# Moving a quarter of each chunk's addition into y from VectorE to TensorE and ScalarE, in the scans of a two-layer kernel

## The chip, the core and the metric

The kernel runs on one core of a Trainium2 chip. The core has a matrix engine (PE, also TensorE; PEld is its loading of weights), a vector engine (DVE, VectorE), a scalar engine (ACT, ScalarE), a general engine (POOL, GpSimd) and a queue engine (SP, SyncE) that mostly starts DMAs. Each engine works through its own queue of instructions in order, and waits on semaphores for the others. The metric is the device time of one execution in microseconds (us). Data lies in SBUF (128 partitions), and TensorE writes its sums into PSUM, eight banks of 512 f32 values per partition.

## The reference, cut to what matters

Two layers run one after the other on an image batch x of 8 x 128 x 128 x 128 (images, height, width, channels). Layer 0 is a linear attention with a layer norm and a residual. Layer 1 projects each image to 256 channels, convolves it depthwise, and runs four selective scans (k = 0 to 3) over its L = 16384 tokens: in order, backwards, in turned order (rows and columns exchanged), and turned backwards. Per scan and channel the recurrence is:

```python
delta = softplus(delta + dbias)
du = delta * u
def step(xc, inp):
    dlt, dut, Bt, Ct = inp
    dA = exp(dlt * A)
    xc = dA * xc + dut * Bt
    return xc, xc * Ct          # D_STATE = 1
y = ys + u * Dv
...
y = y0 + y1 + y2 + y3           # each put back into token order
out = layernorm(y * silu(z)) @ Wout
```

The part that the change touches is the product with C (`xc * Ct`) and the sum of four scans into one y per image.

## The kernel before, in words

The program has three parts: `layer0`, `layer1_front` (projection, convolution, and the rows that make delta, B and C) and `layer1_scan`. Only the last is changed. It works on 512 "units": 8 output images x 4 slots (one scan each) x 16 chunks (`NCH`) of `CH` = 1024 tokens. A chunk has 256 channels, held as two halves c = 0, 1 of 128 partitions. Its tokens fall into two halves of 512 (`hf`). The sums of one image stand in the SBUF tile `y`.

What happens to chunk n, engine by engine:

- `delta(n, c)` (L973): TensorE makes delta for one half of the channels, two bf16 matmuls of 512 columns, into a PSUM tile `px` of two banks. There are three such tiles, taken in turn.
- `soften` (L977): ScalarE takes softplus of it into SBUF (`sp`). `decay` (L981): ScalarE writes exp(A x delta) back over the `px` tile. Softplus and exp lie in different tables of ScalarE, so that a step has two table loads.
- `weigh` (L996; L994 in some steps): POOL multiplies u by delta into `h`. There are two `h` tiles, each for both channel halves of one chunk.
- `scan` (L1004 backwards, L1006 forwards): VectorE runs the recurrence over 1024 tokens, in place in `h`, one instruction per channel half. It starts from the last column of the `h` of the chunk before.
- `spread` (L1012): TensorE spreads C's row over all 128 partitions, one bf16 matmul per token half, into a PSUM bank of its own (tags "pc" and "pt", one bank each).
- `emit(n, hf)`: VectorE multiplies h by C. In the first slot of an image (`place` 0) it writes y directly (L1024). In the other three slots one token half (`sl.first`, the half that holds the scan's last column, which the next chunk's scan still needs) goes into a `px` tile that has become free (L1034 where this slot's order of tokens is turned against y's, L1038 where it isn't), and the other half is multiplied in place in `h` (L1027).
- `gather` (L1046): VectorE adds the product in the `px` tile to y, both channel halves in one instruction.
- `add` (L1054): POOL adds the other token half from `h` to y, one instruction per channel half.

`step(n)` writes out by hand the order in which all this is issued, and `in_order` fixes it: on every engine, instructions run in the order of the text. Step n runs the scans of chunk n, emits chunk n - 1 and makes delta for chunk n + 1. On VectorE a step that only adds ("plain") is `emit`, `gather`, `emit`, `scan` c = 0, `scan` c = 1. On ScalarE it is decay 0, decay 1, softplus 0, softplus 1 (of the next chunk). On TensorE it is delta 0, delta 1, spread, spread. On POOL it is weigh 0, weigh 1, add, add.

While the first slot of the next image runs, the finished image leaves (`leaving`): its chunks are multiplied by the gate, normalised, projected and stored (`gate`, `square`, `moments`, `keep`, `to_tokens`, `square_mean`, `variance`, `deviation`, `project`, `store`), in the same steps. SP's queue starts the loads of u, z and of the rows, POOL's queue adds the u x D terms by DMA (L946).

Of the kernel before, what the change touches and what calls it, by code (L numbers as in the profile page):

```python
# [8 lines left out]
F32 = mybir.dt.float32  # L9
BF16 = mybir.dt.bfloat16  # L10
AF = mybir.ActivationFunctionType
ALU = mybir.AluOpType
# [4 lines left out]
P = 128  # L17
B = 8
H = W = 128
L = H * W  # L20
NH, HD = 4, 32
NC2 = 2
R = 8
K = 4
GW = 4
GN = GW * H
# [4 lines left out]
CH = 1024  # L31
# [757 lines left out]
def layer1_scan(ctx: ExitStack, tc, ubs, xps, zs, gs, dtw, dtb, a_log, gamma, beta, w_out, out):  # L789
# [15 lines left out]
    nc = tc.nc  # L805
    const = ctx.enter_context(tc.tile_pool(name="l2c", bufs=1))
    big = ctx.enter_context(tc.tile_pool(name="l2b", bufs=1))
    wp = ctx.enter_context(tc.tile_pool(name="l2w", bufs=3))
    sm = ctx.enter_context(tc.tile_pool(name="l2s", bufs=4))
    px = ctx.enter_context(tc.tile_pool(name="l2px", bufs=3, space=PSUM))  # L810
    pe = ctx.enter_context(tc.tile_pool(name="l2pe", bufs=1, space=PSUM))
# [14 lines left out]
    for dst, src, rows in ((wparts, dtw.rearrange("k r d -> r k d"), R), (bparts, dtb.rearrange("o (k d) -> o k d", d=D2), 1)):  # L826
        x = wp.tile([rows, K, D2], F32, name="w32", tag="sp", bufs=2)
        nc.sync.dma_start(x, src)
        q = wp.tile([rows, 3, K, D2], BF16, name="w16", tag="h", bufs=2)
# [12 lines left out]
    for i in range(3):  # L842
        t = const.tile([P, CH], BF16, name=f"rows{i}")
# [3 lines left out]
    for i in range(3):  # L847
        t = const.tile([P, D2], BF16, name=f"dtw{i}")
        nc.gpsimd.memset(t, 0.0)
        dws.append(t)  # L850
    csel = const.tile([P, P], BF16, name="csel")
    nc.gpsimd.memset(csel, 0.0)
    nc.gpsimd.memset(csel[96:99, :], 1.0)


    wg = const.tile([P, NC2, P], F32, name="wg")
# [4 lines left out]
    means = wp.tile([P, P], F32, name="means", tag="r", bufs=2)  # L861
    nc.vector.memset(means, 1.0 / (NC2 * P))

    mean = const.tile([P, 32], F32, name="mean2")
    nc.vector.memset(mean, 0.0)
    nc.vector.memset(mean[:, 0:1], 1.0 / (NC2 * P))
    sel = const.tile([P, NC2, 2], F32, name="sel")
    nc.vector.memset(sel, 0.0)
    for j in range(2):
# [65 lines left out]
    units = []  # L935
    for o in range(B):
        for s in ([3, 0, 1, 2] if o % 4 >= 2 else [1, 2, 3, 0]):
            sl = Slot(len(units) // NCH, o, s)
            units += [(sl, i) for i in range(NCH)]

    ubt, sp, da, hs, leaving = {}, {}, {}, {}, {}
# [22 lines left out]
    def delta(n, c):  # L964
        sl, i = units[n]
        rw = rws[n % 3]
        da[n, c] = p = px.tile([P, CH], F32, name="px")
        for hf in range(2):
            if sl.dt_turned_back:
                src = rw[:, (1 - hf) * 512 : (1 - hf) * 512 + 512][:, ::-1]  # L970
            else:
                src = rw[:, hf * 512 : hf * 512 + 512]
            nc.tensor.matmul(p[:, hf * 512 : hf * 512 + 512], sl.dw[:, c * P : c * P + P], src, start=True, stop=True)  # L973

    def soften(n, c):
        sp[n, c] = t = wp.tile([P, CH], F32, name="sp", tag="sp", bufs=2)
        nc.scalar.activation(t, da[n, c], AF.Softplus)  # L977

    def decay(n, c):
        sl, i = units[n]  # L980
        nc.scalar.activation(da[n, c], sp[n, c], AF.Exp, scale=sa[:, sl.s, c : c + 1])  # L981
# [16 lines left out]
    def scan(n, c):  # L998
        sl, i = units[n]
        x, e = da[n, c], hs[n][:, c, :]  # L1000
        last = 0 if sl.back else CH - 1
        start = 0.0 if i == 0 else hs[n - 1][:, c, last : last + 1]
        if sl.back:
            nc.vector.tensor_tensor_scan(e[:, ::-1], x[:, ::-1], e[:, ::-1], start, ALU.mult, ALU.add)  # L1004
        else:
            nc.vector.tensor_tensor_scan(e, x, e, start, ALU.mult, ALU.add)  # L1006

    cps, ts = {}, {}

    def spread(n, hf, tag):  # L1010
        cps[n, hf] = p = pe.tile([P, 1, GN], F32, name="pc", tag=tag)
# [2 lines left out]
    def emit(n, hf):  # L1014

        sl, i = units[n]
        h = hs[n][:, :, hf * 512 : hf * 512 + 512]
        c = cps.pop((n, hf)).to_broadcast([P, NC2, GN])  # L1020
        if sl.place == 0:
            v = sl.y_at(i, hf)
            split = "p c (a b) -> p c a b"
            nc.vector.tensor_tensor(v, h.rearrange(split, b=H), c.rearrange(split, b=H), ALU.mult)  # L1024
            return
        if hf != sl.first:
            nc.vector.tensor_tensor(h, h, c, ALU.mult)  # L1027
            return
        p = da.pop((n, 1))
        if sl.y_turned:  # L1030
            ts[n] = p.rearrange("p (c b a) -> p c b a", c=NC2, a=GW)
            t = p.rearrange("p (c b a) -> p c a b", c=NC2, a=GW)
            split = "p c (a b) -> p c a b"
            nc.vector.tensor_tensor(t, h.rearrange(split, b=H), c.rearrange(split, b=H), ALU.mult)  # L1034
        else:
            t = p.rearrange("p (c q) -> p c q", c=NC2)
            ts[n] = t.rearrange("p c (a b) -> p c a b", b=H)
            nc.vector.tensor_tensor(t, h, c, ALU.mult)  # L1038

    def gather(n):  # L1040

        sl, i = units[n]
        v = sl.y_at(i, sl.first)
        if sl.y_turned:
            v = v.rearrange("p c a b -> p c b a")
        nc.vector.tensor_tensor(v, v, ts.pop(n), ALU.add)  # L1046

    def add(n):
        sl, i = units[n]
        hf = 1 - sl.first  # L1050
        h = hs[n][:, :, hf * 512 : hf * 512 + 512].rearrange("p c (a b) -> p c a b", b=H)
        v = sl.y_at(i, hf)
        for c in range(NC2):
            nc.gpsimd.tensor_tensor(v[:, c], v[:, c], h[:, c], ALU.add)  # L1054


    zt, rst, pts, mv = {}, {}, {}, {}
# [8 lines left out]
    def fetch(o, m):  # L1066
        for hf in range(2):
            zt[m, hf] = z = wp.tile([P, NC2, GN], F32, name="z", bufs=6)
            p = mirrored(o, m, hf)
            nc.sync.dma_start(z, zs[o].rearrange("c p l -> p c l")[:, :, p * GN : p * GN + GN])  # L1070

    def gate(o, m, hf, eng):
        z, ym = zt[m, hf], piece(m, hf)
        eng.tensor_tensor(z, ym[:, :, ::-1] if o % 2 == 1 else ym, z, ALU.mult)  # L1074
# [28 lines left out]
        nc.scalar.activation(t, pts[m][:, :, :, 0], AF.Square)  # L1103

    def variance(m):
        rst[m] = rstd = sm.tile([P, GW, NC2], F32, name="rstd")
        nc.vector.tensor_tensor(rstd, pts.pop(m)[:, :, :, 1], mv.pop(m), ALU.subtract)  # L1107
        nc.vector.tensor_scalar(rstd, rstd, 0.0, EPS1, ALU.max, ALU.add)

# [27 lines left out]
    for o in range(B):  # L1137
        n = (o + 1) * K * NCH
        for j in range(NCH):
# [3 lines left out]
            q = j - LATE if j >= LATE else NCH - LATE + j  # L1143
# [7 lines left out]
    N = len(units)  # L1151

    def step(n):
        live = 0 <= n < N
        then = n + 1 < N
        before = 1 <= n <= N
        now, last, soon, later = (leaving.get(n + i) for i in (0, -1, 1, 2))
        first = before and units[n - 1][0].place == 0
        if before:
            half1 = units[n - 1][0].first  # L1160
            emit(n - 1, half1)
            if not first:
                gather(n - 1)
        if now and last:
            gate(*now, 1, nc.vector)
        if before:
            emit(n - 1, 1 - half1)
        if n + 2 < N:
            load_rows(n + 2)
        if n in fetched:  # L1170
            fetch(*fetched[n])
        if last:
            nc.scalar.preload_act_table_set("natural_log_exp_and_others")
        if live:
            decay(n, 0)
        if now:
            square(now[1], 1)
        if live:
            decay(n, 1)
        if last:  # L1180
            deviation(last[1])
        if live:
            weigh(n, 0)
            if n + 2 < N:
                load(n + 2, 0)
        if live:
            weigh(n, 1)
            if n + 2 < N:
                load(n + 2, 1)
        if now:  # L1190
            moments(now[1])
        if live:
            scan(n, 0)
            da.pop((n, 0))
        if last:
            for hf in range(2):
                store(*last, hf)
        if then:
            for c in range(NC2):
                delta(n + 1, c)  # L1200
        if now:
            keep(now[1])
        if then:
            soften(n + 1, 0)
        if now:
            to_tokens(now[1])
            square_mean(now[1])
        if then:
            soften(n + 1, 1)
        if live:  # L1210
            scan(n, 1)
        if first:
            hs.pop(n - 1)
        if now:
            variance(now[1])
        if live:
            half1 = units[n][0].first
            spread(n, half1, "pc")
            spread(n, 1 - half1, "pt")
        if soon and now:  # L1220
            gate(*soon, 0, nc.gpsimd)
        elif soon:
            gate(*soon, 1, nc.gpsimd)
        elif later:
            gate(*later, 0, nc.gpsimd)
        if soon:
            square(soon[1], 0)
        if now:
            p = da.pop((n, 1)) if live else px.tile([P, CH], F32, name="px")
            for hf in range(2):  # L1230
                project(now[1], hf, p[:, hf * 512 : hf * 512 + 512])
        elif live and units[n][0].place == 0:
            da.pop((n, 1))
        if before and not first:
            add(n - 1)
            hs.pop(n - 1)
        if n in weighed:
            units[weighed[n]][0].weights()
        if n in summed:
            add_d(*summed[n])  # L1240
# [78 lines left out]
```

## Time and profile before

| | before |
|---|---|
| time, three runs | 9049.44, 9056.5 and 9060.8 us, median 9056.5 |
| the profiled execution | 9056.52 us, its span 9054.7 us |
| busy over the span | DVE 89%, POOL 80%, ACT 78%, PE 69% |
| the scan layer | about 4345 to 9050 us of the span |
| L1046, the gather | 384 times, 468.6 us |
| L1054, POOL's add | 768 times, 1162.9 us |

Engines are called by their short names in the profile. A line of a group reads: source line, engine, operation, output<-inputs, shapes, count, then busy time in us, mean ns of one, and the idle time of the engine just before, with what ended it. A line of the timeline reads: start, duration, engine, line, operation, and in brackets the idle time before it. A line of a window reads: busy time (and count) of PE, PEld, DVE, ACT and POOL, the granted share of TensorE's clock, the DMA engines' share and GB/s. L12 is line 12 of the kernel.

### The profile page before, as it was taken

To read this page: it belongs to the slowest core of one execution; us is meant where nothing else is said; L and a number is where in the kernel's file an instruction comes from. 1 tells how busy PE (TensorE), PEld (TensorE's weight loads), DVE (VectorE), ACT (ScalarE), POOL (GpSimd) and SP (SyncE) were. 2 spreads that over 40 slices of the span, in tenths; PEclk is the share of its full clock that TensorE was granted. 3 is DMA by queue.
4 is the path that set the end of the run, shared out by engine and by line. 5 is a ranking of instruction groups with operands and counts; after the bars stand their busy time and mean duration, and the time that the engine had idled before them with its cause. 6 is when DMAs were issued, how large, how long until landed. Compare 5 with 4: busy or idle time off the path is not lost. (4 is left out here: it accounts for less than half of the span.)

```text
span 9054.7 us, 91854 instructions
## 1 busy us (share of the span) xinstructions
PE 6274.4 (69%) x24350; PEld 3062.4 (34%) x24512; DVE 8055.0 (89%) x8337; ACT 7094.7 (78%) x8318; POOL 7222.8 (80%) x4676
## 2 busy tenths in 40 slices
PE   8999999998999999997335437355363453644636
PEld 5656655564333333332003204022040230411303
DVE  6777777777999999998899999999999999999996
ACT  5666666665999999997787888878888888888886
POOL 3656765646789888888698897988979989899796
PEclk9999999999999999999556658566585575755857
DMA  1332323423687888888559678596785876958767
GB/s 78 136 119 112 129 101 149 163 91 140 216 245 251 250 244 244 243 245 251 168 170 254 179 211 243 166 244 192 200 255 154 243 205 188 260 155 226 227 177 211
DMA packets 934775, 1750.71 MB, mean 193 GB/s; under 512 B 150228, under 2 KB 376148, under 8 KB 926064
## 3 DMA queue, kind: packets, MB, share of 16 engines
q1 hardware_dynamic: 873328, 1509.92, 50.6%
q0 software_dynamic: 60928, 234.90, 14.1%
q8 instruction: 200, 3.28, 0.1%
q14 instruction: 319, 2.61, 0.1%
HBM read 1052.36 MB, written 692.12 MB: 193 GB/s over the span
## 5 line engine op out<-in xcount | busy, mean ns | idle before, releaser
L973 PE MATMUL px<-rows,dtw 128*128 128x512 bf16 x1893 | 913.5, 575 | 2291.7 <-DVE y L1046 1079.4
L996 POOL TENSOR_TENSOR h<-ubt,sp 128x1024 f32<-128x1024 f32 x912 | 2173.0, 2413 | 244.6 <-DMA rows<-xps 82.7
L575 DVE SCALAR_TENSOR_TENSOR acc<-xb,cw,acc 128x1024 f32<-128x1024 f32 x1024 | 1320.3, 1289 | 132.9 <-ACT xb L543 89.9
L567 POOL TENSOR_TENSOR tap<-tap 128x1024 f32<-128x1024 f32 x512 | 1223.2, 2392 | 249.1 <-ACT tap L565 225.3
L977 ACT ACTIVATE sp<-px 128x1024 f32<-128x1024 f32 x1024 | 1045.9, 1024 | 434.2 <-PE px L973 383.9
L973 PEld LDWEIGHTS <-dtw 128*128 128x128 bf16 x2048 | 166.0, 110 | 3084.3 <-issue 1016.0
L1006 DVE TENSOR_TENSOR_SCAN h<-px,h 128x1024 f32<-128x1024 f32 x512 | 1178.1, 2332 | 34.4 <-POOL h L996 19.0
L1004 DVE TENSOR_TENSOR_SCAN h<-px,h 128x1024 f32<-128x1024 f32 x512 | 1178.8, 2332 | 24.7 <-POOL h L994 9.5
L1054 POOL TENSOR_TENSOR y<-y,h 128x512 f32<-128x512 f32 x768 | 1162.9, 1561 | 4.0 <-DVE h L1027 4.0
L981 ACT ACTIVATE px<-sp,sa 128x1024 f32<-128x1024 f32 x1024 | 1110.2, 1109 | 6.1
L556 PE MATMUL acc<-xi,wt 128*128 128x512 f32 x2048 | 937.6, 600 | 55.0 <-ACT ures L580 55.0
L565 ACT ACTIVATE tap<-xb,cw 128x1024 f32<-128x1024 f32 x768 | 837.3, 1139 | 14.6 <-POOL xb L540 14.5
L977 ACT ACT_TABLE_LOAD x512 | 656.9, 1283 | 159.3 <-PE px L973 125.5
L994 POOL TENSOR_TENSOR h<-ubt,sp 128x512 f32<-128x512 f32 x224 | 368.0, 1692 | 281.6 <-ACT mv L1103 202.2
L1120 PEld LDWEIGHTS px<-wg,z 128*128 128x128 f32 x4096 | 551.1, 217 | 113.0 <-issue 107.9
L1012 PE MATMUL pc<-rows,csel 128*128 128x512 bf16 x1017 | 514.2, 587 | 83.0 <-DVE rstd L1107 73.9
L556 PEld LDWEIGHTS acc<-xi,wt 128*128 128x128 f32 x2048 | 374.8, 189 | 575.1 <-issue 412.5
L1120 PE MATMUL px<-wg,z 128*128 128x128 f32 x4096 | 551.3, 300 | 0.0
L286 POOL TENSOR_TENSOR q<-q,qs 128x512 f32<-128x512 f32 x256 | 270.3, 1056 | 314.1 <-DVE qs L285 250.0
L981 ACT ACT_TABLE_LOAD x400 | 513.2, 1283 | 7.1
L529 PE MATMUL pxb<-xi,wi 128*128 128x512 f32 x1024 | 496.4, 607 | 3.4 <-ACT xb L538 2.0
L1046 DVE TENSOR_TENSOR y<-y,px 128x1024 f32<-128x1024 f32 x384 | 468.6, 1220 | 14.4
(156 smaller groups left out, 15263.1 us busy)
## 6 DMA issues: line engine op xcount, KB each, us to landing
ubt<-ubs SPq DMA_DIRECT2D x1024, 512.0 KB
zs<-z SPq DMA_DIRECT2D x512, 256.0 KB
ubs<-ures SPq DMA_DIRECT2D x256, 512.0 KB
ubs<-turned SPq DMA_DIRECT2D x256, 512.0 KB
z<-zs SPq DMA_DIRECT2D x256, 512.0 KB
y<-gs POOLq DMA_DIRECT2D x128, 1024.0 KB, 10.1
gs<-du POOLq DMA_DIRECT2D x96, 1024.0 KB, 8.6
rows<-xps SPq DMA_DIRECT2D x1536, 60.0 KB
```

The costliest lines, as they stand in the source:

```text
L556: nc.tensor.matmul(acc[:, s, :], wt[:, j, c, :], x, start=(j == 0), stop=(j == len(ON_PE) - 1))
L565: nc.scalar.activation(t, at(n, c, *d), AF.Copy, scale=weight(n, c, *d))
L567: nc.gpsimd.tensor_tensor(sums[n, c], sums[n, c], t, ALU.add)
L575: nc.vector.scalar_tensor_tensor(acc, at(n, c, *d), weight(n, c, *d), acc, ALU.mult, ALU.add)
L973: nc.tensor.matmul(p[:, hf * 512 : hf * 512 + 512], sl.dw[:, c * P : c * P + P], src, start=True, stop=True)
L977: nc.scalar.activation(t, da[n, c], AF.Softplus)
L981: nc.scalar.activation(da[n, c], sp[n, c], AF.Exp, scale=sa[:, sl.s, c : c + 1])
L996: nc.gpsimd.tensor_tensor(h, u, t, ALU.mult)
L1004: nc.vector.tensor_tensor_scan(e[:, ::-1], x[:, ::-1], e[:, ::-1], start, ALU.mult, ALU.add)
L1006: nc.vector.tensor_tensor_scan(e, x, e, start, ALU.mult, ALU.add)
L1054: nc.gpsimd.tensor_tensor(v[:, c], v[:, c], h[:, c], ALU.add)
L1120: nc.tensor.matmul(po[:, w, :], z[:, c, w * H : w * H + H], wg[:, c, :], start=(c == 0), stop=(c == NC2 - 1))
```

## The change

In the slots that add to y (places 1, 2, 3), the token half that went through a `px` tile is now split by channels. The half c = 0 is done as before: VectorE multiplies into the `px` tile (`emit`) and adds (`gather`), each over 512 instead of 1024 elements. The half c = 1 is multiplied in place in `h` by a new VectorE instruction (`emit_rest`). Then `total` adds it to y on TensorE: two f32 matmuls with an identity as weights, one over y's old values and one over h, into the PSUM bank that held C (tag "pc"). `put_back` copies the sum to y on ScalarE.

Since the last column of h, c = 1, is now overwritten before the next chunk's scan reads it, `hold` copies it out first on ScalarE, and `scan` starts from the copy. `hold` stands behind the first decay in ScalarE's queue. In TensorE's queue `total` stands between the two deltas, in ScalarE's `put_back` stands between the two softplus. `add` on POOL (and `total`, `put_back`) walk the turned chunks in another order: y in runs of four neighbouring elements, h with a step of 128 elements. To make room for the identity, `csel` and `mean` become one column that is spread by a zero step, and `rstd` has two buffers instead of four. The table load and the first decay are written earlier in `step`.

```diff
--- before.py
+++ after.py
@@ -848,9 +848,12 @@
         t = const.tile([P, D2], BF16, name=f"dtw{i}")
         nc.gpsimd.memset(t, 0.0)
         dws.append(t)
-    csel = const.tile([P, P], BF16, name="csel")
+    csel = const.tile([P, 1], BF16, name="csel")
     nc.gpsimd.memset(csel, 0.0)
     nc.gpsimd.memset(csel[96:99, :], 1.0)
+    csel = csel.to_broadcast([P, P])
+    ident = const.tile([P, P], F32, name="ident2")
+    make_identity(nc, ident)
 
 
     wg = const.tile([P, NC2, P], F32, name="wg")
@@ -861,9 +864,9 @@
     means = wp.tile([P, P], F32, name="means", tag="r", bufs=2)
     nc.vector.memset(means, 1.0 / (NC2 * P))
 
-    mean = const.tile([P, 32], F32, name="mean2")
-    nc.vector.memset(mean, 0.0)
-    nc.vector.memset(mean[:, 0:1], 1.0 / (NC2 * P))
+    mean = const.tile([P, 1], F32, name="mean2")
+    nc.vector.memset(mean, 1.0 / (NC2 * P))
+    mean = mean.to_broadcast([P, 32])
     sel = const.tile([P, NC2, 2], F32, name="sel")
     nc.vector.memset(sel, 0.0)
     for j in range(2):
@@ -999,13 +1002,18 @@
         sl, i = units[n]
         x, e = da[n, c], hs[n][:, c, :]
         last = 0 if sl.back else CH - 1
-        start = 0.0 if i == 0 else hs[n - 1][:, c, last : last + 1]
+        if i == 0:
+            start = 0.0
+        elif c and (n - 1) in held:
+            start = held.pop(n - 1)
+        else:
+            start = hs[n - 1][:, c, last : last + 1]
         if sl.back:
             nc.vector.tensor_tensor_scan(e[:, ::-1], x[:, ::-1], e[:, ::-1], start, ALU.mult, ALU.add)
         else:
             nc.vector.tensor_tensor_scan(e, x, e, start, ALU.mult, ALU.add)
 
-    cps, ts = {}, {}
+    cps, ts, cs, held = {}, {}, {}, {}
 
     def spread(n, hf, tag):
         cps[n, hf] = p = pe.tile([P, 1, GN], F32, name="pc", tag=tag)
@@ -1026,24 +1034,52 @@
         if hf != sl.first:
             nc.vector.tensor_tensor(h, h, c, ALU.mult)
             return
-        p = da.pop((n, 1))
+        p = da.pop((n, 1))[:, :GN]
+        h, c = h[:, 0], c[:, 0]
+        cs[n] = c
         if sl.y_turned:
-            ts[n] = p.rearrange("p (c b a) -> p c b a", c=NC2, a=GW)
-            t = p.rearrange("p (c b a) -> p c a b", c=NC2, a=GW)
-            split = "p c (a b) -> p c a b"
+            ts[n] = p.rearrange("p (b a) -> p b a", a=GW)
+            t = p.rearrange("p (b a) -> p a b", a=GW)
+            split = "p (a b) -> p a b"
             nc.vector.tensor_tensor(t, h.rearrange(split, b=H), c.rearrange(split, b=H), ALU.mult)
         else:
-            t = p.rearrange("p (c q) -> p c q", c=NC2)
-            ts[n] = t.rearrange("p c (a b) -> p c a b", b=H)
-            nc.vector.tensor_tensor(t, h, c, ALU.mult)
+            ts[n] = p.rearrange("p (a b) -> p a b", b=H)
+            nc.vector.tensor_tensor(p, h, c, ALU.mult)
+
+    def emit_rest(n):
+
+        h = hs[n][:, 1, units[n][0].first * 512 : units[n][0].first * 512 + 512]
+        nc.vector.tensor_tensor(h, h, cs.pop(n), ALU.mult)
+
+    def hold(n):
+        if n + 1 < N and units[n + 1][1]:
+            last = 0 if units[n][0].back else CH - 1
+            held[n] = t = sm.tile([P, 1], F32, name="held", bufs=2)
+            nc.scalar.copy(t, hs[n][:, 1, last : last + 1])
+
+    def contiguous(n, v):
+        return v.rearrange("p a b -> p b a") if units[n][0].y_turned else v
 
     def gather(n):
 
         sl, i = units[n]
-        v = sl.y_at(i, sl.first)
-        if sl.y_turned:
-            v = v.rearrange("p c a b -> p c b a")
+        v = contiguous(n, sl.y_at(i, sl.first)[:, 0])
         nc.vector.tensor_tensor(v, v, ts.pop(n), ALU.add)
+
+    def total(n):
+
+        sl, i = units[n]
+        hf = sl.first
+        h = hs[n][:, 1, hf * 512 : hf * 512 + 512].rearrange("p (a b) -> p a b", b=H)
+        ts[n, 1] = p = pe.tile([P, GN], F32, name="py", tag="pc")
+        for x in (sl.y_at(i, hf)[:, 1], h):
+            nc.tensor.matmul(p, ident, contiguous(n, x), start=(x is not h), stop=(x is h))
+
+    def put_back(n):
+        sl, i = units[n]
+        v = contiguous(n, sl.y_at(i, sl.first)[:, 1])
+        p = ts.pop((n, 1))
+        nc.scalar.copy(v, p.rearrange("p (b a) -> p b a", a=GW) if sl.y_turned else p.rearrange("p (a b) -> p a b", b=H))
 
     def add(n):
         sl, i = units[n]
@@ -1051,7 +1087,8 @@
         h = hs[n][:, :, hf * 512 : hf * 512 + 512].rearrange("p c (a b) -> p c a b", b=H)
         v = sl.y_at(i, hf)
         for c in range(NC2):
-            nc.gpsimd.tensor_tensor(v[:, c], v[:, c], h[:, c], ALU.add)
+            w = contiguous(n, v[:, c])
+            nc.gpsimd.tensor_tensor(w, w, contiguous(n, h[:, c]), ALU.add)
 
 
     zt, rst, pts, mv = {}, {}, {}, {}
@@ -1103,7 +1140,7 @@
         nc.scalar.activation(t, pts[m][:, :, :, 0], AF.Square)
 
     def variance(m):
-        rst[m] = rstd = sm.tile([P, GW, NC2], F32, name="rstd")
+        rst[m] = rstd = sm.tile([P, GW, NC2], F32, name="rstd", bufs=2)
         nc.vector.tensor_tensor(rstd, pts.pop(m)[:, :, :, 1], mv.pop(m), ALU.subtract)
         nc.vector.tensor_scalar(rstd, rstd, 0.0, EPS1, ALU.max, ALU.add)
 
@@ -1156,6 +1193,13 @@
         before = 1 <= n <= N
         now, last, soon, later = (leaving.get(n + i) for i in (0, -1, 1, 2))
         first = before and units[n - 1][0].place == 0
+        summing = before and not first
+        if last:
+            nc.scalar.preload_act_table_set("natural_log_exp_and_others")
+        if live:
+            decay(n, 0)
+        if summing:
+            hold(n - 1)
         if before:
             half1 = units[n - 1][0].first
             emit(n - 1, half1)
@@ -1165,14 +1209,12 @@
             gate(*now, 1, nc.vector)
         if before:
             emit(n - 1, 1 - half1)
+            if summing:
+                emit_rest(n - 1)
         if n + 2 < N:
             load_rows(n + 2)
         if n in fetched:
             fetch(*fetched[n])
-        if last:
-            nc.scalar.preload_act_table_set("natural_log_exp_and_others")
-        if live:
-            decay(n, 0)
         if now:
             square(now[1], 1)
         if live:
@@ -1196,12 +1238,17 @@
             for hf in range(2):
                 store(*last, hf)
         if then:
-            for c in range(NC2):
-                delta(n + 1, c)
+            delta(n + 1, 0)
+        if summing:
+            total(n - 1)
+        if then:
+            delta(n + 1, 1)
         if now:
             keep(now[1])
         if then:
             soften(n + 1, 0)
+        if summing:
+            put_back(n - 1)
         if now:
             to_tokens(now[1])
             square_mean(now[1])
```

## The prediction

> **What bounds the kernel now.** I read the page's busy times and clock slices first.
>
> ```profile
> PE 6274.4 (69%) x24350; PEld 3062.4 (34%) x24512; DVE 8055.0 (89%) x8337; ACT 7094.7 (78%) x8318; POOL 7222.8 (80%) x4676
> ...
> PEclk9999999999999999999556658566585575755857
> ```
>
> From slice 20 on, the scan layer runs (about 4345 to 9050 us), and TensorE's granted clock falls to 0.5 to 0.8. The page's chain of waits covers only the drain after 8917 us, so I went to a stretch of the layer with nothing but "plain" steps (a chunk is added to y, no chunk leaves), by busy time in a window:
>
> ```profile
> 6211.00:6600.00 389.00, 135.40 (x276) 26.47 (x282) 380.69 (x236) 318.80 (x284) 372.82 (x201) 0.50 0.68 188
> ```
>
> Columns: PE, PEld, DVE, ACT, POOL busy, then the clock. DVE is busy 98%, POOL 96%, ACT 82%, PE 35% at a clock of 0.50. L1054 runs 94 times here, twice a step: 47 steps, 8.28 us each. The timeline of one step:
>
> ```profile
> 6334.20 1.23 DVE L1034 TENSOR_TENSOR px<-h,pc 128x1024 f32<-128x1024 f32 x1
> 6334.33 4.66 POOL L996 TENSOR_TENSOR h<-ubt,sp 128x1024 f32<-128x1024 f32 x2 [0.36 <-DMA rows<-xps]
> 6335.40 2.16 ACT L981 ACTIVATE px<-sp,sa 128x1024 f32<-128x1024 f32 x2
> 6335.47 1.22 DVE L1046 TENSOR_TENSOR y<-y,px 128x1024 f32<-128x1024 f32 x1
> 6336.61 1.21 DVE L1027 TENSOR_TENSOR h<-h,pc 128x1024 f32<-128x1024 f32 x1
> 6336.75 1.04 PE L973 MATMUL px<-rows,dtw 128*128 128x512 bf16 x2 [2.94 <-DVE y L1046]
> 6337.74 4.46 DVE L1004 TENSOR_TENSOR_SCAN h<-px,h 128x1024 f32<-128x1024 f32 x2
> 6337.88 1.28 ACT L977 ACT_TABLE_LOAD   x1 [0.32 <-PE px L973]
> 6338.96 3.24 POOL L1054 TENSOR_TENSOR y<-y,h 128x512 f32<-128x512 f32 x2
> 6339.18 1.02 ACT L977 ACTIVATE sp<-px 128x1024 f32<-128x1024 f32 x1
> 6340.08 1.03 PE L973 MATMUL px<-rows,dtw 128*128 128x512 bf16 x2 [2.29 <-DVE h L1004]
> 6341.23 1.02 ACT L977 ACTIVATE sp<-px 128x1024 f32<-128x1024 f32 x1 [1.03 <-PE px L973]
> 6342.27 1.28 ACT L981 ACT_TABLE_LOAD   x1
> 6342.30 1.23 DVE L1034 TENSOR_TENSOR px<-h,pc 128x1024 f32<-128x1024 f32 x1
> ```
>
> The reader is to see that DVE's five instructions stand end to end (L1034, L1046, L1027, two scans) and set the step. The ACT order matters later: second softplus, table load, first decay; that decay would end near 6344.7, and the next scan, which needs it, starts near 6345.9. ACT has 1.2 us of slack there.
>
> Prices of the new operations, by group, and f32 matmuls of 512 columns at a granted 0.50, then at 1.00, from the timeline of the layer before:
>
> ```profile
> L300 DVE TENSOR_TENSOR o<-po,bb 128x512 f32<-128x512 f32 x256 | 173.6, 678 | 7.7 <-PE po L298 7.5
> L1093 ACT COPY sr<-pm 128x512 f32<-128x512 f32 x128 | 74.9, 585 | 145.2 <-PE pm L1087 145.2
> L225 ACT ACTIVATE a<-a 128x1 f32<-128x1 f32 x56 | 11.0, 197 | 2.6 <-DVE a L216 2.6
> L647 ACT COPY turned<-ures 128x512 f32<-128x512 f32 x96 | 104.5, 1089 | 0.0
> ```
>
> ```profile
> 2239.16 4.20 PE L556 MATMUL acc<-xi,wt 128*128 128x512 f32 x5 [5.48 <-ACT ures L580]
> ...
> 2301.59 3.70 PE L556 MATMUL acc<-xi,wt 128*128 128x512 f32 x8 [0.54 <-ACT ures L580]
> ```
>
> An f32 matmul is two such instructions (L556 asks for 1024 and 2048 are counted), each 4.20/5 = 0.84 us at 0.50 and 3.70/8 = 0.46 at 1.00.
>
> **The change, part by part** (384 chunks are added to y; 376 of them in plain steps, 8 in the first step of a leaving slot).
>
> *DVE.* The first product and the gather halve: 1.23 and 1.22 become 0.68 each (L300). The new `emit_rest` adds 0.68. Balance by durations -0.41 us; by starts (DVE's neighbours overlap by about 0.08 us) -0.5. DVE's own order would take 8.28 - 0.5 = 7.8 us.
>
> *ACT.* `put_back` 0.585 (L1093; its turned writes are runs of four, which cost DVE's L1046 nothing: 1.22 like the rest; upper end L647's 1.09). `hold` 0.20 (L225). The rows L1093 show copies without a table load. ACT's sum: two loads 2.56, two decays 2.16, two softplus 2.04, 0.79: 7.55. Alone, it fits.
>
> *POOL.* `add` walks y and h in another order in turned chunks. Now 1.62; lower end 1.25 (the least of L1054), upper 2.2 (its most). I take 1.62, as the same elements move: 4.66 + 3.24 = 7.9 us a step, hidden as long as a step is longer. At 2.2 POOL needs 9.1.
>
> *TensorE.* `total` is two f32 matmuls, four instructions: 4 x 0.84 = 3.36 us at 0.50, 4 x 0.46 = 1.85 at 1.00. Which clock? A step's work then is 1.0 + 3.4 + 1.0 + 1.1 = 6.5 of some 9 us at the low clock, a share of 0.7; were the full clock granted, it would fall to about 0.4, near the 0.35 that this stretch gets 0.50 for. So full speed doesn't hold itself; and `total` begins after a pause of PE. I take 0.50. By the Trainium skill ("TensorE: Matmul & The Clock Gate", Part 1) a busy window of about 3.4 us lifts the clock from 1.2 to 2.4 GHz: estimated so, `total` would pass slowly and only the delta after it at full speed, which makes some 9150 of this forecast; the row of this stretch stands by 0.50, no run here shows a `total`.
>
> *The new loop.* `total` stands in PE's queue ahead of the delta for the second half of channels; it waits for `emit_rest` (which reads C's bank and writes the h that is added). `emit_rest` waits for `hold`, and `hold` stands in ACT's queue behind the decay, which follows that delta's softplus. So, once a step:
>
> emit_rest 0.68, total 3.36, delta 1.03 (L973), softplus 1.02, table load 1.28, decay 1.06 (a pair takes 2.16, so its successor starts 1.06 after it), hold 0.20: 8.63. Hand-overs, read off the timeline: DVE to PE 0.06 (6336.69 to 6336.75), PE to ACT 0.12 (6341.11 to 6341.23), ACT to DVE about 0.05, four of 0.02 within: 0.3. Together 8.93 us, over DVE's 7.8, POOL's 7.9, ACT's 7.55. `put_back` (0.585) runs beside the delta (1.03) and C's spread, which waits for it, beside softplus. Plain steps: 376 x (8.93 - 8.28) = +244.
>
> *The 8 others.* Same loop, with `keep` (0.585) and the moments in front: +1.5 each, an estimate from 0.65 + 0.585 and hand-overs; ends 0 and 4 (a whole `total`): +12.
>
> *Edits at nothing.* On ACT the decay's new place is the old order (only DVE's instructions lay between); no DMA moves, and SP's and POOL's loads of later chunks come no earlier. The one-column `csel` and `mean` are spread by a zero step, as L601's weights are: 189 ns, like L556's 189, loaded beside running matmuls; without that cover 2 x 0.15 a step. The extra identity is about 0.5 us of POOL (0.20 + 0.29 in the earlier layers) in a set-up that waits for DMAs until 4343 us. Two rstd buffers suffice: one is written after the store of the one before.
>
> Sum: +256. The profiled execution took 9056.52 us (span 9054.7), which is the median of the runs: 9057 + 256 = 9313, so 9310.
>
> **The rivals.**
>
> *Faster: the clock is granted.* At 1.00 the loop loses 1.51 (`total`) and 0.45 (delta): 7.0, and POOL's 7.9 sets the step: 376 x -0.38 + 12 = -131, 8925; with POOL's adds at 1.25, DVE's 7.8: 8890. It decides once `total` and delta lose 0.65 of 4.39, a clock of 0.59 over them. For: from 6600 to 6640 us PE is busy 75% and gets 0.85. Against: the share above halves with it.
>
> *Partly granted:* delta at full speed, or a tail of `total`: 8.4 to 8.7, 9115 to 9230.
>
> *Slower still: a strided read on PE.* In the 256 turned chunks `total` reads h 512 bytes apart. ACT's copy so read takes 1089 against 585 ns (L647, L1093), 1.86 times. By that ratio the h half (1.68) costs 1.44 more: 256 x 1.44 = +369, 9680. Lower end nothing: DVE reads so at its usual pace, and L647 with 1024 elements takes 1921, so 0.83 us for 512 more, no more than the 0.84 PE needs at 0.50. I take nothing, as that row is a rate and PE is slow. If y's runs of four slowed too, 10050. The skill ("SBUF — State Buffer", the note on cachelines in "Door 1: The DMA port swizzle") says that each access to a new 16-byte line pays a penalty; it speaks against this reading order, gives no price, and agrees with L647, not with DVE.
>
> *put_back at 1.09:* it outlasts the delta by about 0.25 in turned chunks: +64, 9375.
>
> **How the numbers follow.** Low clock and cheap reads 0.57 (own range 9230 to 9400), strided reads dear 0.14 (9400 to 9780), partly granted 0.11, no change 0.03 (within 0.2%, about what a measurement can tell), faster 0.15. So slower 0.82. To leave out no more than 2 in 10, the range runs from 9040, with the faster case outside, to 9780.
>
> **What would show it.** Plain steps near 8.9 us; DVE's share below 90%, idle before `emit_rest`, released by ACT's `hold`; the second delta released behind `total`, not by a scan; `total`'s four instructions over 3.4 us; PE's share about doubled with the clock still near 0.5. Steps of 7.8 with DVE at 98% would make it wrong, as would a clock of 0.6 or more over `total`, or `total` not waiting for `emit_rest`.

## The result, and the profile after

The changed kernel is slower: a median of 9201.72 us over four runs against 9058.65 us, a ratio of 1.0157 (95% interval 1.014 to 1.0174), or about +143 us. One of the four took 10603.58 us at a granted clock of 0.67, against 0.88 in the other three, and the ratio leaves it out. Its profiled execution took 9202.39 us, its span is 9200.6 us.

The page of the changed kernel, busy times and clock:

```profile
PE 7293.8 (79%) x26048; PEld 3472.9 (38%) x26048; DVE 7896.0 (86%) x8720; ACT 7339.4 (80%) x9062; POOL 7160.2 (78%) x4678
...
PEclk9999999999999999997679778787787787877878
```

VectorE did lose work (8055.0 to 7896.0 us busy) and TensorE took on some 1000 us (6274.4 to 7293.8), yet the span grew by 145.9. VectorE's share of the span fell from 89% to 86%: it now waits. TensorE's clock rose from 0.5 to 0.8 over the scan layer to 0.6 to 0.9.

Where the time went can be counted from the ends of each chunk's first scan in the two traces:

| steps | count | before, us | after, us | difference |
|---|---|---|---|---|
| plain steps that add to y | 376 | 3119 (8.29 each) | 3267 (8.69 each) | +148 |
| first step of a leaving slot | 7 | 75 | 73 | -2 |
| steps of the first slots | 128 | 1371 | 1371 | 0 |
| drain after the last scan | | 135.2 | 136.8 | +2 |

So it is all in the plain steps (the first scan itself ends 1.8 us earlier). Those that add turned chunks (256) grew by 0.45 us on average, the others by 0.27. A stretch of such steps, by window (busy PE, PEld, DVE, ACT, POOL, clock, DMA share, GB/s), and VectorE's two longest waits in it:

```profile
6300.00:6550.00 250.00, 159.82 (x291) 49.73 (x290) 223.10 (x175) 215.08 (x230) 222.55 (x118) 0.74 0.55 161
```

```profile
DVE h L1052 <- ACT held L1058: 14.8, 27, 0.9
DVE px L1044 <- PE pc L1020: 9.0, 19, 0.8
```

VectorE is busy 89% of this stretch, where it was 98%. It waits for two things that were not there before: `emit_rest` (L1052) waits for `hold` (L1058) 27 times in 29 steps, and the first product (L1044) waits for the spread of C, which stands behind `put_back`. Two rounds of the same kernel show what decides how long a step is. The first, in a turned chunk, has `total` and the delta at half the clock; timeline from one `emit_rest` to the next:

```profile
4504.93 0.69 DVE L1052 TENSOR_TENSOR h<-h,pc 128x512 f32<-128x512 f32 x1 [0.57 <-ACT held L1058]
...
4505.67 2.07 PE L1076 MATMUL py<-y,ident 128*128 128x512 f32 x2 [1.80 <-DVE h L1052]
...
4507.54 1.93 PE L1076 MATMUL py<-h,ident 128*128 128x512 f32 x2
...
4509.29 1.03 PE L976 MATMUL px<-rows,dtw 128*128 128x512 bf16 x2
4509.50 0.58 ACT L1082 COPY y<-py 128x512 f32<-128x512 f32 x1 [1.25 <-PE py L1076]
...
4510.44 1.02 ACT L980 ACTIVATE sp<-px 128x1024 f32<-128x1024 f32 x1 [0.35 <-PE px L976]
...
4511.48 1.28 ACT L984 ACT_TABLE_LOAD   x1
...
4512.77 1.12 ACT L984 ACTIVATE px<-sp,sa 128x1024 f32<-128x1024 f32 x1
4513.83 0.17 ACT L1058 COPY held<-h 128x1 f32<-128x1 f32 x1
...
4514.03 0.69 DVE L1052 TENSOR_TENSOR h<-h,pc 128x512 f32<-128x512 f32 x1 [0.70 <-ACT held L1058]
```

Apart from `put_back` (L1082), which runs beside the loop, every line here starts when the one before it is done: `emit_rest`, `total` (3.62 us from its first matmul to the delta behind it), delta, softplus, table load, decay, `hold`, `emit_rest`. The round takes 9.10 us. The second, in a chunk that isn't turned, runs with `total` at the full clock:

```profile
4767.96 0.69 DVE L1052 TENSOR_TENSOR h<-h,pc 128x512 f32<-128x512 f32 x1 [0.51 <-ACT held L1058]
...
4768.71 1.12 PE L1076 MATMUL py<-y,ident 128*128 128x512 f32 x2 [1.74 <-DVE h L1052]
...
4769.67 1.02 PE L1076 MATMUL py<-h,ident 128*128 128x512 f32 x2
...
4775.07 0.17 ACT L1058 COPY held<-h 128x1 f32<-128x1 f32 x1
...
4775.73 0.68 DVE L1052 TENSOR_TENSOR h<-h,pc 128x512 f32<-128x512 f32 x1
```

The round takes 7.77 us, and `hold` is done 0.5 us before `emit_rest`: VectorE's own order is the bound again. Sorted by the granted clock over the 5.5 us after the start of `emit_rest`, the rounds of the whole trace average 9.04 us (129 rounds at or below 0.52), 8.55 (156 between 0.6 and 0.7), 8.14 (33 between 0.7 and 0.8) and 7.76 (28 above 0.9, of which 26 in chunks that aren't turned). The kernel before averages 8.29 per plain step.

### The profile page after: what moved, and what is told of

The parts are those of the page before. It is cut to its first block, busy times and chain, and to the rows that moved or that the text cites. A ratio compares the mean times of both kernels' runs of the same rounds, so it can differ in the third digit from the quotient of the medians.

```text
span 9200.6 us, 95629 instructions
## 1 busy us (share of the span) xinstructions
PE 7293.8 (79%) x26048; PEld 3472.9 (38%) x26048; DVE 7896.0 (86%) x8720; ACT 7339.4 (80%) x9062; POOL 7160.2 (78%) x4678
## 5 line engine op out<-in xcount | busy, mean ns | idle before, releaser
L976 PE MATMUL px<-rows,dtw 128*128 128x512 bf16 x2048 | 745.2, 452 | 766.5 <-DVE y L1067 474.9
L1076 PE MATMUL py<-y,ident 128*128 128x512 f32 x768 | 708.0, 1021 | 637.3 <-DVE h L1052 633.4
L984 ACT ACTIVATE px<-sp,sa 128x1024 f32<-128x1024 f32 x1024 | 1136.4, 1112 | 6.1
L980 ACT ACTIVATE sp<-px 128x1024 f32<-128x1024 f32 x1024 | 1046.6, 1024 | 81.6 <-PE px L976 71.2
L1091 POOL TENSOR_TENSOR y<-y,h 128x512 f32<-128x512 f32 x768 | 1106.9, 1489 | 0.0
L976 PEld LDWEIGHTS <-dtw 128*128 128x128 bf16 x2048 | 216.5, 111 | 1611.3 <-issue 1350.4
L1014 DVE TENSOR_TENSOR_SCAN h<-px,h 128x1024 f32<-128x1024 f32 x332 | 774.7, 2338 | 31.8 <-ACT px L984 18.7
L1012 DVE TENSOR_TENSOR_SCAN h<-px,h 128x1024 f32<-128x1024 f32 x332 | 775.4, 2338 | 23.2 <-POOL h L997 9.4
L1076 PE MATMUL py<-h,ident 128*128 128x512 f32 x768 | 699.7, 1004 | 0.0
L1082 ACT COPY y<-py 128x512 f32<-128x512 f32 x384 | 224.6, 585 | 383.2 <-PE py L1076 383.0
```

What stands on the lines that cost most here:

```text
L1076: nc.tensor.matmul(p, ident, contiguous(n, x), start=(x is not h), stop=(x is h))
L1091: nc.gpsimd.tensor_tensor(w, w, contiguous(n, h[:, c]), ALU.add)
```

## The experiments

All are edits of the changed kernel, and ratios are against the kernel before. Where a number of the expectations speaks of theory A, it is the loop above; B to F are its rivals, G adds what the clock does to the loop, and H is G's rival.

**hold ahead of the first decay.**

```diff
+        if summing:
+            hold(n - 1)
         if live:
             decay(n, 0)
-        if summing:
-            hold(n - 1)
```

> Only hold and the first decay change places in ScalarE's queue. Theory A (the loop emit_rest, total, second delta, second softplus, table load, first decay, hold, emit_rest sets the step): the decay and the wait behind it leave the loop; what is left is the chain emit_rest, total, put_back, spread of C, first product, gather, other product, emit_rest, 0.69 + 3.41 + 0.3 + 0.59 + 0.06 + 0.43 + 0.3 + 0.7 + 0.6 + 1.13 = 8.2 us at the low clock, less where the clock is granted: plain steps 8.1 to 8.3 against 8.7 after the change, 9010 to 9060 us. Rival B (VectorE is simply slowed by other work on SBUF and PSUM, or ScalarE's added copies fill its queue): no change, 9200 us.

Measured: 8995.3 us, ratio 0.9928 (0.9913 to 0.9943). A copy of one column that changes places with one activation gives back 206 us, and the kernel is then faster than before the change. Plain steps average 8.14 us (3060 us for 376). VectorE's waits from 6250 to 6450 us, which is plain steps:

```profile
DVE px L1044 <- PE pc L1020: 6.5, 12, 0.8
DVE h L1012 <- ACT px L984: 1.3, 4, 0.4
```

The wait for `hold` is gone, the one for C's spread is left. Theory A holds. The time is a little under the range given (9010 to 9060); the clock over `total` rose too, from 0.60 to 0.65, which may be why. Rival B falls: the copies on ScalarE are all still there.

**total without y's old values.**

```diff
-        for x in (sl.y_at(i, hf)[:, 1], h):
-            nc.tensor.matmul(p, ident, contiguous(n, x), start=(x is not h), stop=(x is h))
+        for x in (h,):
+            nc.tensor.matmul(p, ident, contiguous(n, x), start=True, stop=True)
```

> Leaves out part of the computation: total passes only h through the identity, without y's old values, so that one of the two f32 matmuls is gone; put_back, hold and all waits stay. Theory A: the loop loses 1.71 us at the low clock and falls below VectorE's own order, plain steps 7.7 to 7.9 us, 8860 to 8920 us. Rival B (the copies on ScalarE, not total's length): 9150 to 9200 us.

Measured: 8913.25 us, ratio 0.9836 (0.9816 to 0.9855). The median plain step is 7.75 us, the mean 7.88, at a clock of only 0.51 over `total`. From 6250 to 6450 us VectorE hardly waits for `hold`:

```profile
DVE h L1052 <- ACT held L1058: 0.2, 1, 0.2
```

So the length of `total` is what closes the loop, and 7.75 us is what VectorE's new order costs.

**hold first, and VectorE's order turned.** The other token half is multiplied first, so that the product which needs the late spread of C comes later. Beside the edit of the first experiment:

```diff
+            if summing:
+                emit(n - 1, 1 - half1)
             emit(n - 1, half1)
             if not first:
                 gather(n - 1)
...
-            emit(n - 1, 1 - half1)
             if summing:
                 emit_rest(n - 1)
+            else:
+                emit(n - 1, 1 - half1)
...
-            spread(n, half1, "pc")
-            spread(n, 1 - half1, "pt")
+            if units[n][0].place:
+                spread(n, 1 - half1, "pt")
+                spread(n, half1, "pc")
+            else:
+                spread(n, half1, "pc")
+                spread(n, 1 - half1, "pt")
```

> hold ahead of the first decay, and in the added slots VectorE multiplies the other token half first (its spread of C comes first too), so that the first product, which waits for put_back and the spread behind it, comes 1.13 us later. Theory A: both loops are cut, the longest left is emit_rest, total, put_back, spread, first product, gather, emit_rest, 7.1 us at the low clock; VectorE's own order, 7.7 to 7.8 us, or POOL's 7.7 sets the step: 8860 to 8920 us, faster than before the change. Rival B: 9150 to 9200 us. Rival C (only hold's place counts, the rest is bound by something else): as the run with hold alone.

Measured: 8958.99 us, ratio 0.9885 (0.9869 to 0.9902), 36 us below `hold` alone and 40 to 100 above what was expected. Plain steps average 8.05 us, not 7.75. What I had missed stands in VectorE's waits (6250 to 6450 us):

```profile
DVE h L1012 <- ACT px L984: 1.9, 8, 0.3
DVE h L1035 <- PE pc L1020: 1.8, 3, 0.7
```

L1035, the product moved to the front, now waits for its own spread, since that stands in TensorE's queue behind `total` and the second delta as well. As long is the other wait, of the first scan for ScalarE's decay: from 4500 to 9000 us they come to 31.2 us and 31.4. And 7.75 is a median; the median here is 7.89.

**VectorE's order turned, hold left where it was.** The same edit on the changed kernel itself.

> The other half of the pair: VectorE's new order (other token half first, its spread first) with hold left behind the first decay. Theory A: the loop through the second delta, softplus, table load, decay and hold is untouched, plain steps stay near 8.7 us, 9180 to 9230 us. Rival E (the first product's wait for the spread of C behind put_back is the harm, and hold's place gave little): near the run with both, 8960 to 9050 us.

Measured: 9239.45 us, ratio 1.0203 (1.0183 to 1.0224), about 38 us slower than the change and a little above the range. VectorE's wait is the old one:

```profile
DVE h L1052 <- ACT held L1058: 13.3, 17, 0.9
DVE h L1035 <- PE pc L1020: 6.7, 11, 0.7
```

Without `hold` first, the turned order gives nothing; rival E falls. (The clock over `total` was 0.56 here, against 0.60.)

**total behind the second delta.**

```diff
             delta(n + 1, 0)
+            delta(n + 1, 1)
         if summing:
             total(n - 1)
-        if then:
-            delta(n + 1, 1)
...
-        if summing:
-            put_back(n - 1)
...
             soften(n + 1, 1)
+        if summing:
+            put_back(n - 1)
```

> total behind the second delta in TensorE's queue, put_back behind the second softplus. Rival D (the harm is that total stands ahead of the second delta): the delta comes when its scan ends, and the kernel gets faster than 9100 us. Theory A: total then starts only after the first scan and the delta, and a longer loop closes: emit_rest 0.69, scan 2.34, delta 0.85, total 3.41, put_back 0.59, table load 1.29, decay 1.06, hold 0.2 and hand-overs, 10.8 us at the low clock and 8.7 at full, so slower: 9350 to 9900 us.

Measured: 10029.72 us, ratio 1.1068 (1.1045 to 1.109). As a remedy, rival D's move fails by far: freeing the delta costs another 828 us. That `total` did no harm ahead of the second delta isn't shown by it, since the loop of theory A runs through that place too. The time is above the range that I gave (9350 to 9900), and the loop that closed is not the one that I wrote down. VectorE's longest wait from 6250 to 6450 us:

```profile
DVE px L1047 <- PE pc L1020: 37.7, 14, 3.3
```

By this wait, the loop is the one through C's bank: `emit_rest`, first scan, delta, `total`, `put_back`, spread of C, first product, gather, other product. Plain steps took 10.36 us where the slot's order isn't turned and 11.00 where it is.

**The early spread ahead of total.** `hold` first, the turned order, and in plain steps this:

```diff
             delta(n + 1, 0)
+        early = summing and live and units[n][0].place and not now
+        if early:
+            spread(n, 1 - units[n][0].first, "pt")
         if summing:
             total(n - 1)
...
-                spread(n, 1 - half1, "pt")
+                if not early:
+                    spread(n, 1 - half1, "pt")
```

> As the run with hold first and the new order, and the spread of C for the half that VectorE multiplies first goes ahead of total in TensorE's queue (in plain steps). Its plain steps took 8.05 us where VectorE's order takes 7.75; theory A: the rest is that this spread stood behind total and the second delta, 0.69 + 3.41 + 0.85 + 0.43 + 0.3 + 1.2 + 0.7 + 0.7 = 8.3 us at the low clock. With it early the steps fall to 7.75 to 7.8 us: 8840 to 8880 us. Rival F (POOL, which waits for total to release h): no change, 8950 us.

Measured: 9011.89 us, ratio 0.9948 (0.9931 to 0.9964): 53 us slower than without it, and my expectation was wrong. VectorE no longer waits for a spread of C at all; it waits for ScalarE's decay (118.7 us from 4500 to 9000 us, where it was 31.4):

```profile
DVE h L1012 <- ACT px L984: 8.8, 15, 1.1
```

`total` now starts after one more matmul, and what depends on it late in the step (second delta, softplus, table load, decay, the next scan) comes later. That this chain over two steps is what bounds the last two kernels is argued from this wait; no run takes it apart. Rival F is not borne out: in this stretch POOL isn't what VectorE waits for.

**More matmuls.** The clock is the other half of the theory, and it can be raised by giving TensorE more to do. Both repeats write the same values again.

```diff
-            nc.tensor.matmul(p[:, hf * 512 : hf * 512 + 512], sl.dw[:, c * P : c * P + P], src, start=True, stop=True)
+            for _ in range(2 if c == 0 and n and units[n - 1][0].place else 1):
+                nc.tensor.matmul(p[:, hf * 512 : hf * 512 + 512], sl.dw[:, c * P : c * P + P], src, start=True, stop=True)
...
-        nc.tensor.matmul(p[:, 0, :], csel, rws[n % 3][:, hf * 512 : hf * 512 + 512], start=True, stop=True)
+        for _ in range(5 if tag == "pt" and units[n][0].place else 1):
+            nc.tensor.matmul(p[:, 0, :], csel, rws[n % 3][:, hf * 512 : hf * 512 + 512], start=True, stop=True)
```

> The changed kernel with more work on TensorE and nothing else: the delta for the first half of channels is made twice, the spread of the half with a bank of its own five times, six bf16 matmuls more a step, 2.6 us at the low clock and 1.3 at full, all outside the stretch from emit_rest to the second delta. Theory G (the size of the loop is set by the granted clock over total, which follows TensorE's busy share): the clock over total rises from 0.60 to 0.75 or more, and the kernel gets faster in spite of the added work, 9000 to 9150 us. Rival H (the clock over total does not follow, or the added work delays the queue): 9200 to 9400 us.

Measured: 8938.76 us, ratio 0.9871 (0.9851 to 0.9891): 263 us less than the changed kernel, with more work and no wait taken away. The same 1000 us of the two traces by window, the changed kernel first:

```profile
5500.00:6500.00 1000.00, 692.50 (x2608) 321.57 (x2607) 902.24 (x908) 852.42 (x965) 835.17 (x443) 0.80 0.69 199
```

```profile
5500.00:6500.00 1000.00, 744.82 (x2949) 335.91 (x3003) 957.57 (x923) 907.22 (x1021) 906.36 (x485) 0.95 0.71 209
```

The clock goes from 0.80 to 0.95 (over `total` alone from 0.60 to 0.90), VectorE from 90% to 96% busy. Plain steps average 8.00 us, 7.76 in the median. Theory G holds, and the time lies below the range that I gave for it (9000 to 9150).

**Both remedies.** `hold` first and the repeated matmuls.

> Both remedies in one: hold ahead of the first decay, and the six repeated bf16 matmuls a step. Theories A and G together: at a clock near 0.9 over total and without decay in the loop, plain steps fall to VectorE's own 7.75 us but for the steps still at the low clock, about 7.85: 8,860 to 8,920 us, below either remedy alone (8,995 and 8,939 us). Rival: both remedies free the same time, and the sum is that of the better one, 8,930 to 8,950 us.

Measured: 8909.38 us, ratio 0.9838 (0.9822 to 0.9855), the fastest kernel here with the full computation: 145 us below the kernel before (9053.98 us beside it) and 292 below the change. Plain steps average 7.91 us, 7.75 or little over in the median. The gains overlap, as they must where both shorten the same loop towards VectorE's 7.75: 206 and 263 us alone, 292 together.

## Why the prediction was right or wrong

The direction was right and so was the mechanism, down to the engines and their order; 9201.72 us lies in the range, 108 below the forecast of 9310. Point by point:

- *The new loop* (8.93 us at the low clock): right. The round quoted above takes 9.10, and rounds at the low clock average 9.04. The difference is mostly `total`, 3.62 us up to the delta, where I had 3.36. `hold` first, which takes the decay out, and the halved `total` each removed the wait.
- *`put_back` and the spread of C, "beside softplus"*: put at nothing, and a second chain all the same. From 4500 to 9000 us VectorE's first products waited 131.8 us for the spread, against 194.5 us in which `emit_rest` waited for `hold`. In a round that waits for `hold` anyway it adds little, by the sum of the loop; with `hold` first it is what is left, at 8.14 us a step.
- *"Which clock? ... I take 0.50"*: this is the step that failed. The clock over `total` averaged 0.60, on the edge of what the prediction itself named as a sign of being wrong. The share of 0.7 at the low clock, falling to about 0.4 at full, was the right sum; what I drew from it was wrong. It doesn't keep the clock low, it makes it swing: the trace of before has 128 stretches of constant clock, that of after 810, many of them 3.41 us long. Of 376 plain steps some ran at 9.0 us and some at 7.8, with a mean of 8.69: +0.40 us a step against the +0.65 forecast, +148 us for +244.
- *"It decides ... a clock of 0.59"*, of the faster rival: wrong as a test. At 0.60 over `total` the kernel was still slower, for two reasons. A mean clock doesn't give a mean duration when the clock swings: in the 128 chunks that aren't turned it averaged 0.65, and yet `total` took 3.23 us on average, 60 times about 3.78 at the low clock and 32 times about 1.96 at the full one. And in the 256 turned chunks (0.58 and 3.59 us) `total` takes 2.86 us even at the full clock, because h is read with a step (next section but one), so that the rival's loop of 7.0 us doesn't come about there. That the rival's 8925 lies near the 8939 of the run with more matmuls, at 0.90, is partly luck: POOL's 7.9 didn't set its steps, VectorE's 7.76 did in the median, and in the turned round from 4487.25 to 4495.01 us `hold` is done only 0.04 us before `emit_rest` starts.
- *"Partly granted: 9115 to 9230"*, a rival at 0.11, is the case that came true. The Trainium skill's rule ("TensorE: Matmul & The Clock Gate", Part 1), that a busy window of about 3.4 us lifts the clock, gave an estimate of 9150 and was nearer than the row that I preferred. The traces agree with that rule in part: every rise of the clock in the scan layer, 56 before and 398 after, follows a 3.41 us stretch in which PE's records fill 77% or more. But 14 stretches before and 12 after, filled to 80% or more, left the clock low; there the measurement decides, and why is open.
- *VectorE's order, 7.8 us*: right, 7.75 to 7.77 where nothing else binds. `put_back` at 0.585 and `hold` at 0.20: measured 0.585 and 0.174. `put_back`'s turned writes cost nothing.
- *POOL's add, taken at 1.62 us*: 1.51 in the turned stretch, where the trace of before has about 1.64; hidden either way.
- *The 8 others, +12 us*: wrong by sign, 7 of them together changed by -2. In those steps `total` ran at the full clock in six of eight, in 1.88 us. That the matmuls of the moments, ahead of it, raise the clock, and that this is why, is argued, not shown.
- *Slower still, a strided read on PE* (0.14): not at the low clock, where the interval between two h matmuls is 0.88 us in turned chunks and 0.85 in the others. At the full clock it is real (next section but one), and the changed kernel had a share of that; what it cost there no run takes apart. The note in "SBUF — State Buffer" that spoke against this order is borne out there, and not at the low clock.

## What to carry to other kernels

Moving work off the busiest engine puts a chain through other engines' queues in its place; write that chain down as a loop, with every instruction that stands ahead of a waiting one, and compare its round with the time per step. An instruction that someone waits for belongs ahead of whatever doesn't need it: the one-column copy behind a decay cost 206 us. When the loop goes through TensorE, its price hangs on the granted clock, which can swing between two prices, as it did here, rather than stay at either; a mean clock then says little.

## What the runs showed of the hardware that was not expected

Repeating six bf16 matmuls per step, with no other use, made the kernel 263 us faster: the loop through TensorE was paid at the granted clock (0.60 over `total` before, 0.90 with the repeats), and the clock rose with the time that TensorE was busy (692.50 to 744.82 us of 1000). In the changed kernel it is also seen to rise only after stretches of 3.41 us that were at least 79% busy (12 that were 80% or more didn't raise it), and to fall after ones that were at most 71% busy; it stayed up after some as low as 45%.

An f32 matmul whose moving operand is read with a step of 512 bytes doesn't profit from the full clock. `total` in the kernel with more matmuls (L1078 there), both at a granted 1.00, first in a turned chunk (y in runs of four elements, h 512 bytes apart), then in one that isn't:

```profile
4487.99 1.13 PE L1078 MATMUL py<-y,ident 128*128 128x512 f32 x2 [0.77 <-DVE h L1054]
4488.95 1.90 PE L1078 MATMUL py<-h,ident 128*128 128x512 f32 x2
```

```profile
4742.16 1.13 PE L1078 MATMUL py<-y,ident 128*128 128x512 f32 x2 [0.71 <-DVE h L1054]
4743.13 1.02 PE L1078 MATMUL py<-h,ident 128*128 128x512 f32 x2
```

The pair over y takes 1.13 us in both, so runs of four cost nothing. The pair over h takes 1.90 against 1.02: the interval between its two instructions is 0.85 us, which is what it is at the low clock (0.85 to 0.88), instead of 0.43.
